# A smaller last group with paired down products, several chunks per bank, and identity products spread over the steps, in an LSTM with a mixture of experts

## The chip, the core and the metric

The kernel runs on one core of a Trainium2 chip. TensorE (PE) multiplies matrices and writes its results to PSUM, VectorE (DVE) and ScalarE (ACT) read them there, and SyncE (SP) issues most DMAs. Each engine works through its own instructions in the order in which the program issues them, and waits for the others by semaphores. The profile has two rows for TensorE: PE for the matmuls, and PEld for the loads of their stationary operand. An fp32 matmul is recorded as two passes, each with its own load, so a count of passes is twice the count of products.

The metric is the device time of one execution in microseconds (us). It is given as the median of several runs.

## What is computed

Two stages follow each other, each with a residual sum. The first is an LSTM over 1024 steps for two sequences of width 256:

```python
xW = einsum('ntd,dk->tnk', x, Wx) + b
def step((h, c), xw_t):
    a = xw_t + h @ Wh                       # 2 x 1024
    i, f, o = sigmoid(a[:, :256]), sigmoid(a[:, 256:512]), sigmoid(a[:, 512:768])
    g = tanh(a[:, 768:])
    c = f * c + i * g
    h = o * tanh(c)
x = x + hs
```

The second treats each of the 2 x 1024 tokens by itself. Two shared experts have a hidden width of 512, and eight routed experts a hidden width of 256. A router chooses two of the eight for each token:

```python
shared = sum_e (silu(x @ s_w1[e].T) * (x @ s_w3[e].T)) @ s_w2[e].T / 2
s = sigmoid(concat(x, cond) @ W_router.T)   # eight scores per token
idx = top_k(s + router_bias, 2)
gates = s[idx] / sum(s[idx])                # spread over the eight experts, zero elsewhere
routed = sum_e gelu(x @ r_w1[e].T) @ r_w2[e].T * gates[:, e]
x = x + (shared + routed) / 4
```

## The kernel before

**The recurrence.** One pass of the loop over `t` (L626) is one step. L641 to L651 issue 32 products of the last h with `Wh`, 64 columns each, on four column strips of the array (`ROWS` = 32): 64 passes. They accumulate onto the input part of the gates, which stands in the bank already. Then follow, for each of the two halves `m` of the hidden units, a transpose on DVE (L672), the sigmoids and the tanh on ACT (L675, L676), the cell on DVE (L679 to L684), its tanh on ACT (L692), and h on DVE (L695). The next step's first products need the first half of h.

**The input part.** `queue_inputs` (L531) queues products of x with `Wx` for 128 steps at a time (`XB`), and ACT moves them to SBUF with the bias. `inject` (L554) puts them into the gates' banks with identity products. A bank serves eight steps (`TH`). After the last burst of eight steps (`ahead`, L652) both banks of the next eight get their four identity products each: eight products, 16 passes, in one step.

**The experts as filler.** The tokens' work is done beside the recurrence, a group of steps later. `GROUPS` (L35) cuts the 1024 steps into seven groups of 128 and two of 64. When the last step of a group is done, `experts(t0, S)` (L255) queues its units on `fill.pe`. In the order of the queue they are: the router's scores, the up products of shared and routed experts, then per 128 tokens the identity product that brings in x with the shared down products, and the routed down products. A unit is mostly one matmul. `PACES` (L37) says in how many steps after the group's end its units are to be done. Each step runs at most `ROOM` = 2 of them behind its burst (L657, L658), less when fewer suffice for the due step:

```python
left = max(1, due - t)
done = fill.run_pe(min(ROOM - ahead, -(-len(fill.pe) // left)))
```

A unit that opens a PSUM bank runs only while a bank is free. There are two (`FILL_BANKS`, L38), and a bank is given back when the DVE operation that reads it last is issued (`let_go`). If a step has run fewer units than its room, padding follows (L659 to L664): products of the identity with itself, 256 columns, whose result nobody reads.

What ACT and DVE do for the experts stands in two more queues. `fill.run(fill.act, 1.0)` (L709) and `fill.run_dve(0.5)` (L718) take from them, in a step, as much as a written cost allows. The router's choice is some twenty small DVE operations in a queue `aside`, at a cost of `ASIDE` = 0.18 each.

**Chunks and banks.** An up product's bank holds two chunks of 128 hidden units, whatever the group's size: `w1` and `w3` of one chunk for the shared experts (`shared_up`, L363), and two chunks of `r1` for the routed ones (`routed_up`, L385).

**The end.** The last group ends with the last step, so nothing is left to hide its work. After L723 the queues are emptied, four more banks are lent to the filler (`fill.last`), and `drain` (L735) issues the group of 64 steps, 128 tokens. Its up products are cut into four strips of 32 output rows (`up_product`, L354). It has 8 shared and 16 routed down products of 256 columns, one identity product unit, and one sum on DVE per expert (`add_expert`, L446). An output DMA closes it.

Of the kernel before, what the change touches and what calls it, by code (L numbers as in the profile page):

```python
# [32 lines left out]
TOP_K = 2  # L33

GROUPS = [128] * 7 + [64] * 2  # L35

PACES = [128] * 6 + [84, 60, 0]  # L37
# [4 lines left out]
ROOM = 2  # L42
ASIDE = 0.18
# [67 lines left out]
def lstm_moe_kernel(  # L111
# [91 lines left out]
    nc.vector.tensor_scalar(ident_s, ident, 1.0 / SHARED, None, ALU.mult)  # L203
    rev = const.tile([P, E], F32, name="rev")
# [50 lines left out]
    def experts(t0, S):  # L255

        W = N * S
        NT = W // P
        mov = [x2[:, k, N * t0 : N * t0 + W] for k in range(K)]
        st = {}  # L260
        piece = 0.4 if W > P else 0.25

        def lhs(k, i):
            return toks(mov[k], i)

        def toks(a, i):
            return a[:, i * P : (i + 1) * P]


        def scores(i):  # L270
            if i == 0:
                st["lg"] = bank()[:, :, :E]
            for k in range(K):
                nc.tensor.matmul(
                    st["lg"][:, i, :], lhs(k, i), wr_sb[:, k, :],
                    start=(k == 0), stop=(k == K - 1),
                )
            if i == NT - 1:
                fill.to_dve(0.2, add_condition)

        def big(name):
            return route.tile([P, NT, E], F32, name=name)

        def small(name):
            return route.tile([P, NT], F32, name=name)

        def wide(a):
            return a.unsqueeze(2).to_broadcast([P, NT, E])

        def add_condition():  # L290
            st["z"] = big("z")
            nc.vector.tensor_add(
                st["z"], st["lg"][:, :NT, :], cond_lg.unsqueeze(1).to_broadcast([P, NT, E])
            )
            fill.let_go()
            fill.to_act(0.25, squash, lag=1)
# [6 lines left out]
        def choose():  # L303

            s = st["s"]
            rev_w = rev.unsqueeze(1).to_broadcast([P, NT, E])
# [3 lines left out]
                sel0, s, rb_sb.unsqueeze(1).to_broadcast([P, NT, E]), ALU.add))  # L310
# [39 lines left out]
            ]  # L350
            return ops


        def up_product(ps, half, w, c, k):  # L354

            rows = ROWS if fill.last and W <= P else P
            for r in range(0, P, rows):
                nc.tensor.matmul(  # L358
                    ps[r : r + rows, half, :W], w[:, k, c * P + r : c * P + r + rows], mov[k],
                    start=(k == 0), stop=(k == K - 1), skip_group_check=True,  # L360
                )

        def shared_up(c, i):  # L363
            if i == 0:
                if c == 0:
                    st["h_s"] = hidden.tile([P, NS * HS // P, N * P], F32, name="h_s")
                st["up"] = bank()
            up_product(st["up"], i // K, w3_sb if i // K else w1_sb, c, i % K)
            if i == 2 * K - 1:
                ps = st["up"]  # L370
                fill.to_act(0.4, lambda: shared_act(c, ps))

        def shared_act(c, ps):
            sg = work.tile([P, N * P], F32, name="sg")
            nc.scalar.activation(sg[:, :W], ps[:, 0, :W], AF.Sigmoid)
            y = work.tile([P, N * P], F32, name="y")
            fill.to_dve(piece, lambda: nc.vector.tensor_mul(y[:, :W], ps[:, 0, :W], sg[:, :W]))
            fill.to_dve(piece, lambda: shared_gate(c, ps, y))

        def shared_gate(c, ps, y):  # L380
            nc.vector.tensor_mul(st["h_s"][:, c, :W], ps[:, 1, :W], y[:, :W])
            fill.let_go()

        def routed_up(c2, i):
            if i == 0:  # L385
                if c2 == 0:
                    st["h_r"] = hidden.tile([P, E * HR // P, N * P], F32, name="h_r")
                st["up"] = bank()
            up_product(st["up"], i // K, r1_sb, 2 * c2 + i // K, i % K)
            if i == 2 * K - 1:  # L390
                ps = st["up"]
                fill.to_act(0.65, lambda: routed_act(c2, ps))

        def routed_act(c2, ps):
            er = work.tile([P, 2, N * P], F32, name="er")
            nc.scalar.activation(er[:, :, :W], ps[:, :, :W], AF.Erf, scale=RSQRT2)
            for half in range(2):
                fill.to_dve(piece, lambda half=half: routed_gate(c2, half, ps, er))

        def routed_gate(c2, half, ps, er):  # L400
            nc.vector.scalar_tensor_tensor(
                st["h_r"][:, 2 * c2 + half, :W], er[:, half, :W], 1.0, ps[:, half, :W],
                ALU.add, ALU.mult,
            )
            if half:
                fill.let_go()


        def shared_down(i, c):
            if c < 0:  # L410
                st["down"] = bank()
                x_kqj = st["down"][:, 0, :].rearrange("p (q k j) -> p k q j", q=Q, k=K)
                for k in range(K):
                    nc.tensor.matmul(
                        x_kqj[:, k], lhs(k, i), ident_s,
                        start=(k == 0), stop=False, skip_group_check=True,
                    )
                return
            last = c == NS * HS // P - 1
            nc.tensor.matmul(  # L420
                st["down"][:, 0, :], toks(st["h_s"][:, c, :], i), w2_sb[:, c, :],
                start=False, stop=last, skip_group_check=True,
            )
            if last:
                ps = st["down"]
                fill.to_dve(0.45, lambda: begin_sum(i, ps))

        def begin_sum(i, ps):
            st["acc", i] = work.tile([P, D], F32, name="acc")
            nc.vector.tensor_scalar(st["acc", i], ps[:, 0, :], SHARED, None, ALU.mult)  # L430
            fill.let_go()

        def routed_down(i, e2, j):
            if j == 0:
                st["down"] = bank()
            ps, half, h = st["down"], j // (HR // P), j % (HR // P)
            c = (2 * e2 + half) * (HR // P) + h
            nc.tensor.matmul(  # L438
                ps[:, half, :], toks(st["h_r"][:, c, :], i), r2_sb[:, c, :],
                start=(h == 0), stop=(h == HR // P - 1), skip_group_check=True,  # L440
            )
            if j == 2 * (HR // P) - 1:
                for half in range(2):
                    fill.to_dve(0.5, lambda half=half: add_expert(i, 2 * e2 + half, ps[:, half, :]), late=True)

        def add_expert(i, e, ps):  # L446
# [6 lines left out]
            if e == E - 1:  # L453
                t = t0 + i * (P // N)
                nc.sync.dma_start(out=out_tn[t : t + P // N], in_=acc)
# [3 lines left out]
        for c in range(NS * HS // P):  # L459
            units += [(int(i == 0), lambda c=c, i=i: shared_up(c, i)) for i in range(2 * K)]  # L460
        for c2 in range(E * HR // P // 2):
            units += [(int(i == 0), lambda c2=c2, i=i: routed_up(c2, i)) for i in range(2 * K)]
# [91 lines left out]
    def inject(ps, m, grp):  # L554
        blk, g = divmod(grp, XB // TH)
        assert all((blk, 4 * m + i, g * PAIR) in made for i in range(4))
        for q in range(Q):
            nc.tensor.matmul(  # L558
                ps[q * ROWS : (q + 1) * ROWS],
                pairs(blk)[:, 2 * m + q // 2, g].rearrange("p c r -> p (c r)"),  # L560
                ident[:, q % 2 * 64 : q % 2 * 64 + 64],
                start=True, stop=False, skip_group_check=True,
            )
# [59 lines left out]
    for m in range(K):  # L623
        inject(nxt[m][0], m, 0)
    due = 0
    for t in range(T):  # L626
        fill.step = t
        grp, u = divmod(t, TB)
        if t % TH == 0:
            cur, nxt = nxt, [gates_tile(m) for m in range(K)]  # L630
            ps, turned, busy = [a[0] for a in cur], [a[1] for a in cur], nxt[0][2]
            fresh = True
# [4 lines left out]
        if t == XB // 2:  # L637
            queue_inputs(1)

# [12 lines left out]
        ahead = t + 1 < T and t % TH == TH - 1  # L652
        if ahead:
            for m in range(K):
                inject(nxt[m][0], m, (t + 1) // TH)
            fresh = False
        left = max(1, due - t)  # L657
        done = fill.run_pe(min(ROOM - ahead, -(-len(fill.pe) // left)))  # L658
        for _ in range((ROOM if t < XB else 1) - done - ahead):  # L659
            nc.tensor.matmul(  # L660
                busy, ident, ident.unsqueeze(1).to_broadcast([P, 2, P]),
                start=fresh, stop=False, skip_group_check=True,
            )
            fresh = False  # L664
# [48 lines left out]
        if t == 2 * TB:  # L713
            lg = bank()[:, 0, :E]
            fill.banks -= 1
            fill.pe.extend((0, lambda k=k: condition_scores(lg, k)) for k in range(K))
        if u < TB - 1:
            fill.run_dve(0.5)  # L718
            continue
        residual(grp, int(grp == 0 or t - TB in ends), TB)  # L720
        if t in ends:
# [6 lines left out]
            if (t + 1) % XB == 0 and t + 1 + XB < T:  # L728
                queue_inputs((t + 1) // XB + 1)
# [82 lines left out]
```

## Time and profile before

The median of three runs is 2267.33 us (2264.34 to 2267.87).

| | |
|---|---|
| profiled execution, device time | 2267.39 us |
| its span, first to last instruction | 2265.6 us |
| mean granted TensorE clock | 0.998 |
| PE busy | 1923.0 us (85%) |
| PEld busy | 1417.4 us (63%) |
| DVE busy | 1571.0 us (69%) |
| ACT busy | 910.3 us (40%) |
| L644, the products with `Wh`, 65,536 passes | 1136.0 us of PE |
| L672, the transposes | 543.8 us of DVE, 266 ns each |
| L660, padding, 430 passes | 124.7 us of PE |
| L558, identity products, 2048 passes | 56.2 us of PE |

The busy share of PE is an average over 1024 steps that all have the same shape. Matmuls are pipelined, and the time of a row contains their latency, so 85% does not say that PE is full. What a change is worth must be read within one step, from where PE begins its filler to where the next burst can start, and from the steps that are longer than the others. The time from the last h to the end of the span, in which only the last group works, is read by itself.

### The profile page before, as it was taken

The numbers are of one execution on the slowest core, as the hardware profiler recorded it, in microseconds if no ns is written. First come the engines' busy times: TensorE is split into PE (matmuls) and PEld (weight loads), VectorE is DVE, ScalarE is ACT, GpSimd is POOL, SyncE is SP. The second block draws the span as 40 slices with busy tenths as digits, with TensorE's granted clock in tenths as the row PEclk, the third lists the DMA queues.
The fourth block names the chain that finished last, engine by engine and source line by source line (L and its number), as shares of the span: only waits on it lengthen the run. The fifth ranks groups of instructions, "written<-read, shape, count | busy, mean of one in ns | idle before, by whom it ended". The sixth has DMA issues, their size and how long they took to land.

```text
span 2265.6 us, 159453 instructions
## 1 busy us (share of the span) xinstructions
PE 1923.0 (85%) x70844; PEld 1417.4 (63%) x70844; DVE 1571.0 (69%) x10992; ACT 910.3 (40%) x6499; POOL 2.7 (0%) x9
## 2 busy tenths in 40 slices
PE   9999988888888888888888888888888888898888
PEld 6777765555655556555655556655566555676667
DVE  5666667766776667776677766776667766777776
ACT  4343344433444334443444434444343443343342
POOL 0000000000000000000000000000000000000000
PEclk9999999999999999999999999999999999999999
DMA  1221000000000000000000000000000000000000
GB/s 60 69 60 32 5 5 5 4 5 7 7 5 4 4 7 7 4 5 7 7 4 5 4 7 7 5 4 4 7 7 4 4 5 7 7 5 7 7 5 8
DMA packets 10707, 23.85 MB, mean 11 GB/s; under 512 B 2080, under 2 KB 7712, under 8 KB 10016
## 3 DMA queue, kind: packets, MB, share of 16 engines
q1 hardware_dynamic: 9728, 12.61, 1.9%
q8 instruction: 553, 9.06, 1.6%
q14 instruction: 138, 1.13, 0.2%
q10 hardware_dynamic: 288, 1.05, 0.1%
HBM read 11.56 MB, written 2.10 MB: 6 GB/s over the span
## 4 chain that ended last, share of the span: by engine, by line
PE 62%; DVE 34%; issue 3%; DMA 0%; SPq 0%; ACT 0%
PE ps L644 52%; DVE ps L672 10%; DVE c L684 9%; DVE results L679 7%; DVE seen L683 6%; PE ps L660 5%; DVE h L695 3%; PE ps_f L358 2%; PE ps_f L524 2%; PE ps_f L438 1%; PE ps_f L420 0%; PE ps L358 0%; DMA wh_sb<-in_wh_dram 0%; PE ps L558 0%; PE ps L438 0%
## 5 line engine op out<-in xcount | busy, mean ns | idle before, releaser
L644 PEld LDWEIGHTS ps<-wh_sb,h 128*32 128x32 f32 x65536 | 966.5, 110 | 727.7 <-DVE h L695 715.4
L644 PE MATMUL ps<-wh_sb,h 128*32 128x64 f32 x65536 | 1136.0, 221 | 331.7 <-DVE h L695 322.9
L672 DVE STREAM_TRANSPOSE ps<-ps 128x64 f32<-128x64 f32 x2048 | 543.8, 266 | 503.7 <-PE ps L644 433.9
L675 ACT ACTIVATE results<-ps 128x6 f32<-128x6 f32 x2048 | 362.9, 177 | 1106.0 <-DVE ps L672 1004.4
L695 DVE TENSOR_TENSOR h<-results,c 128x2 f32<-128x2 f32 x2048 | 313.6, 153 | 168.1 <-ACT c L692 168.0
L692 ACT ACTIVATE c<-c 128x2 f32<-128x2 f32 x2048 | 321.5, 157 | 218.0 <-DVE c L684 181.6
L684 DVE TENSOR_TENSOR_SCAN c<-results 128x4 f32<-128x4 f32 x2048 | 358.0, 175 | 0.0
L676 ACT ACTIVATE results<-ps 128x2 f32<-128x2 f32 x2048 | 340.3, 166 | 0.0
L683 DVE COPY seen<-results 128x2 f32<-128x2 f32 x2048 | 332.1, 162 | 0.0
L679 DVE TENSOR_TENSOR results<-results,c 128x2 f32<-128x2 f32 x2048 | 319.4, 156 | 0.0
L358 PE MATMUL ps_f<-x2T,w_sb 128*128 128x256 f32 (+2 forms) x608 | 168.7, 392 | 0.0
L358 PE MATMUL ps_f<-x2T,r_sb 128*128 128x256 f32 (+2 forms) x608 | 167.8, 390 | 0.0
L438 PE MATMUL ps_f<-r_sb,h_r 128*128 128x256 f32 x488 | 164.7, 426 | 0.0
L660 PE MATMUL ps<-ident 128*128 128x256 f32 x430 | 124.7, 408 | 0.8 <-issue 0.8
L358 PEld LDWEIGHTS ps_f<-x2T,w_sb 128*128 128x128 f32 (+1 forms) x608 | 79.2, 176 | 21.6 <-issue 0.3
L358 PEld LDWEIGHTS ps_f<-x2T,r_sb 128*128 128x128 f32 (+1 forms) x608 | 79.0, 176 | 21.5
L438 PEld LDWEIGHTS ps_f<-r_sb,h_r 128*128 128x128 f32 x488 | 74.4, 188 | 21.5
L660 PEld LDWEIGHTS ps<-ident 128*128 128x128 f32 x430 | 72.0, 189 | 16.8 <-issue 1.1
L420 PE MATMUL ps_f<-w_sb,h_s 128*128 128x256 f32 x240 | 81.5, 427 | 0.0
L524 PE MATMUL ps_f<-xT_sb,wx_sb 128*128 128x256 f32 (+2 forms) x384 | 78.6, 340 | 0.5 <-ACT inputs L513 0.3
L448 DVE SCALAR_TENSOR_TENSOR acc<-ps_f,gate,acc 128x256 f32<-128x256 f32 x122 | 58.3, 478 | 0.8 <-PE ps_f L438 0.7
L558 PE MATMUL ps<-ident,inputs 128*32 128x64 f32 x2048 | 56.2, 219 | 2.7 <-issue 2.0
(83 smaller groups left out, 498.9 us busy)
## 6 DMA issues: line engine op xcount, KB each, us to landing
r_sb<-in_r_w1T_dram SPq DMA_DIRECT2D x4, 512.0 KB, 3.8
r_sb<-in_r_w2T_dram SPq DMA_DIRECT2D x4, 512.0 KB, 4.5
out_dram<-acc SPq DMA_DIRECT2D x16, 128.0 KB, 2.8
xT_sb<-in_xT_dram SPq DMA_DIRECT2D x6, 256.0 KB, 2.9
wx_sb<-in_wx_dram ACTq DMA_DIRECT2D x2, 512.0 KB, 4.5
wh_sb<-in_wh_dram SPq DMA_DIRECT2D x2, 512.0 KB, 6.3
w_sb<-in_s_w1T_dram SPq DMA_DIRECT2D x2, 512.0 KB, 4.2
w_sb<-in_s_w3T_dram SPq DMA_DIRECT2D x2, 512.0 KB, 4.0
```

Source lines behind the costliest of these rows:

```text
L358: nc.tensor.matmul(ps[r : r + rows, half, :W], w[:, k, c * P + r : c * P + r + rows], mov[k], start=(k == 0), stop=(k == K - 1), skip_grou ...
L438: nc.tensor.matmul(ps[:, half, :], toks(st["h_r"][:, c, :], i), r2_sb[:, c, :], start=(h == 0), stop=(h == HR // P - 1), skip_group_check= ...
L644: nc.tensor.matmul(ps[m][q * ROWS : (q + 1) * ROWS], h_window(t, k, pair), wh_sb[:, k, w0 : w0 + 64], start=False, stop=(t % TH == TH - 1 ...
L660: nc.tensor.matmul(busy, ident, ident.unsqueeze(1).to_broadcast([P, 2, P]), start=fresh, stop=False, skip_group_check=True,)
L672: nc.vector.transpose(turned[m], ps[m])
L675: nc.scalar.activation(sgm[:, u, m, :, :, 1], gates[m][:, 0:3], AF.Sigmoid)
L676: nc.scalar.activation(gf[:, u, m, :, 0], gates[m][:, 3], AF.Tanh)
L679: nc.vector.tensor_mul(gf[:, u, m, :, 1], sgm[:, u, m, 2, :, 1], c_prev[m][:, :, 1])
L683: nc.vector.tensor_copy(seen[m], gf[:, u, m, :, 0])
L684: nc.vector.tensor_tensor_scan(c_new[m].rearrange("p n z -> p (n z)"), sgm[:, u, m, 0].rearrange("p n z -> p (n z)"), gf[:, u, m].rearrang ...
L692: nc.scalar.activation(cells[m][:, 2, :, 0], c_new[m][:, :, 1], AF.Tanh)
L695: nc.vector.tensor_mul(h_cols(t + 1)[:, m], sgm[:, u, m, 1, :, 1], cells[m][:, 2, :, 0])
```

## The change

Several edits come together.

**Groups.** A group of 32 steps is put in after the third group, and the last two groups have 64 and 32 steps. `XB` stays at 128, so the input products are queued at multiples of 128 steps, now apart from the groups' ends. The paces change with the groups: the last full group is due in 56 steps, the group of 64 in 31.

```diff
-GROUPS = [128] * 7 + [64] * 2
-PACES = [128] * 6 + [84, 60, 0]
+GROUPS = [128] * 3 + [32] + [128] * 4 + [64, LAST]
+PACES = [128] * 7 + [56, 31, 0]
-ROOM = 2
-ASIDE = 0.18
+ROOM = 3
+ASIDE = 0.19
```

**Identity products and padding.** Each step issues one of the eight identity products behind its filler. Padding is one product a step, and only in the eight steps of a bank whose first step had no filler. The input products of the first two blocks get due steps (12 and 128).

```diff
-        ahead = t + 1 < T and t % TH == TH - 1
-        if ahead:
-            for m in range(K):
-                inject(nxt[m][0], m, (t + 1) // TH)
-            fresh = False
         left = max(1, due - t)
-        done = fill.run_pe(min(ROOM - ahead, -(-len(fill.pe) // left)))
-        for _ in range((ROOM if t < XB else 1) - done - ahead):
+        done = fill.run_pe(min(ROOM, -(-len(fill.pe) // left)))
+        if t % TH == 0:
+            spare = not done
+        if spare and not done:
             nc.tensor.matmul(busy, ident, ...)
+        if t // TH + 1 < T // TH:
+            inject(nxt, t // TH + 1, t % TH)
...
-            fill.run_dve(0.5)
+            fill.run_dve(0.6)
```

**Several chunks per bank.** `up` takes the place of `up_product`, `shared_up` and `routed_up`. A bank holds `C` = 512 / W chunks for W tokens: two for a group of 128 steps, four for 64, eight for 32. All its products are 128 output rows by W columns, in the last group too. ACT and DVE then take half a bank at once, 256 columns, whatever W is.

```diff
+        C = 2 * 256 // W
+        def up(b, j):
+            i, k = divmod(j, K)
+            w, c = r1_sb, b * C - 2 * NS * HS // P + i
+            if c < 0:
+                w, c = (w1_sb, w3_sb)[i // (C // 2)], b * C // 2 + i % (C // 2)
...
+            nc.tensor.matmul(
+                ps[:, i, :], w[:, k, c * P : (c + 1) * P], mov[k],
+                start=(k == 0), stop=(k == K - 1), skip_group_check=True,
+            )
```

**The last group in pairs.** The last group has 64 tokens, half of the array's columns. Its scores are computed twice, for rows 0 to 63 and 64 to 127. Two chunks of a shared expert, or two experts, have their down products on the two halves of the array, and one DVE sum adds both with a gate per row. At the end a product with `fold` (two identities above each other) adds the two halves, ACT copies the result, and one DMA writes it.

```diff
+        def last_routed_down(e2):
+            ps = bank()
+            for h in range(HR // P):
+                for g in range(2):
+                    c = (2 * e2 + g) * (HR // P) + h
+                    nc.tensor.matmul(
+                        ps[g * W : (g + 1) * W, 0, :], st["h_r"][:, c, :W], r2_sb[:, c, :],
+                        start=(h == 0), stop=(h == HR // P - 1), skip_group_check=True,
+                    )
+            fill.to_dve(0.5, lambda: last_add(e2, ps), lag=0, late=True)
+
+        def last_add(e2, ps):
+            acc = st["acc", 0]
+            nc.vector.scalar_tensor_tensor(
+                acc, ps[:, 0, :], st["gates"][:, e2 : e2 + 1], acc, ALU.mult, ALU.add
+            )
+            fill.let_go()
+            if e2 == E // 2 - 1:
+                both = bank()[:W, 0, :]
+                nc.tensor.matmul(both, fold, acc, start=True, stop=True)
+                total = work.tile([P, D], F32, name="y")[:W]
+                nc.scalar.activation(total, both, AF.Copy)
+                nc.sync.dma_start(out=out_tn[t0 : t0 + S], in_=total)
```

`last_shared_down` does the same for the shared experts' eight chunks. One of the last two residual sums, which make the tokens from h, is issued before the last burst instead of behind it.

## Prediction

> **What bounds the kernel now.** I read the chain of waits first, then the matmuls in order of time, the table of waits, and last the granted clock in single windows. The chain:
>
> ```profile
> PE 62%; DVE 34%; issue 3%; DMA 0%; SPq 0%; ACT 0%
> ```
>
> Its largest line is the 64 passes of L644, which I call a burst: the product of one step with Wh. The recurrence h → burst → transpose → gates → h is the bound, and everything else has to fit beside it. In order of time, on PE:
>
> ```profile
> 2200.01 1.10 PE L644 MATMUL ps<-wh_sb,h 128*32 128x64 f32 x64 [0.19 <-DVE h L695]
> 2201.04 1.13 PE L420 MATMUL ps_f<-w_sb,h_s 128*128 128x256 f32 x4
> 2202.16 1.10 PE L644 MATMUL ps<-wh_sb,h 128*32 128x64 f32 x64
> ```
>
> Columns: start, time, engine, line, operation, operands, passes. A step takes 2.155 us. Filler can start 1.03 us into it, and two products of 256 columns (two passes each) still fit. Steps are this regular except in 45 places. The two writes of h in a step (L695) run from 11.4 to 2234.6, so 1023 steps take 2222.9 us; 1023 x 2.1545 is 2204.0, so about 18.3 us (summed over the 45) are lost. Where:
>
> ```profile
> PEld ps L644 <- issue: 10.7, 21, 0.9
> PEld ps L558 <- issue: 4.5, 12, 0.8
> ...
> 633.67 1.10 PE L644 MATMUL ps<-wh_sb,h 128*32 128x64 f32 x64 [0.43 <-DVE h L695]
> 634.59 0.41 PE L558 MATMUL ps<-ident,inputs 128*32 128x64 f32 x16
> 634.92 0.70 PE L358 MATMUL ps_f<-x2T,w_sb 128*128 128x256 f32 x2
> 635.83 1.09 PE L644 MATMUL ps<-wh_sb,h 128*32 128x64 f32 x61 [0.20 <-DVE h L695]
> 637.45 0.30 PE L644 MATMUL ps<-wh_sb,h 128*32 128x64 f32 x3 [0.54 <-issue]
> ...
> q8 instruction: 553, 9.06, 1.6%
> ```
>
> The burst stops three passes before its end with nothing to wait for. PE and PEld have 70,844 instructions each; 9.06 MB over them is 64 bytes each, and 553 packets make blocks of 16 KB, 256 instructions. All stops of this kind in L644 fall on the same place modulo 256: PE waits for the next block. Two regular steps hold about 264 instructions, so a block lasts some 4.2 us. The step before this stop had the eight identity products (L558, 16 passes): a block begun early in its burst is used up 2.8 us later, and its successor arrives 3.3 to 3.8 us after the begin. Two stretches are of another kind:
>
> ```profile
> 1425.50:1428.90 3.40, 2.37 (x88) 2.10 (x92) 2.42 (x19) 1.55 (x12) 0.00 (x0) 1.00 0.02 5
> 1428.90:1432.40 3.50, 3.50 (x103) 2.68 (x95) 1.46 (x12) 0.79 (x6) 0.00 (x0) 0.51 0.02 5
> 1705.40:1708.80 3.40, 3.25 (x77) 2.43 (x81) 1.60 (x14) 0.95 (x7) 0.00 (x0) 0.51 0.02 5
> ```
>
> The seventh number after the stretch's length (0.51) is the granted clock: twice PE ran at half speed for 3.4 us, each time after a step or two whose only filler was the 8-column router products (L274). The four steps touched lost 0.64, 0.42, 0.86 and 0.12, 2.04 us together. So 16.2 us belong to blocks of instructions: 5.5 before step 130, 10.7 later.
>
> **Identity products, one per step.** Their number stays. No step has 16 extra passes any more; with one filler product a step is 136 instructions, with two 140. I walked the block borders through the new order of PE. A border now moves back 16 to 24 instructions every two steps, and where it enters the head of a burst the next one lies at the end of the following burst, 3.0 us on. The trace has such pairs (steps 149, 181, 397) without a stop[...]. So the late 10.7 us go. Of the early 5.5 some 4 stay: there the weights' DMAs delay the blocks, and they are loaded at the same steps. **-12.2 us.** A rule speaks against this: the Trainium skill, "Runtime: NRT & Kernel Launch", section "Instruction fetch mechanics", has the crossing of a 16 KiB block mostly hidden. By it this part is worth nothing and the sum below ends at 2284.2; the row shows stops, so I take the row.
>
> **Up to three filler products per step** (ROOM 3, the new paces). The new order has 780 steps with one wide product, 92 with two, and 31 with three (or the router's four and one) plus an identity product, nearly all from 928 to 983, where 128 steps' work is due within 56 and two banks make a pattern of three, one, three, one. Another five or six (1015 to 1022) have three without identity product. What does a third cost? A late filler that holds the burst up:
>
> ```profile
> 670.59 0.70 PE L358 MATMUL ps_f<-x2T,r_sb 128*128 128x256 f32 x2
> 671.22 1.10 PE L644 MATMUL ps<-wh_sb,h 128*32 128x64 f32 x64
> ```
>
> From its start to the burst: 0.63 us, with h ready 0.12 earlier. A further product adds two passes of 0.216 (L420's 16 passes take 3.46 in the chain). Three: 1.03 + 0.63 + 4 x 0.216 = 2.52, and 0.04 for the identity product (16 passes of L558 take 0.41), 2.56: 0.41 over 2.155. 31 x 0.41 + 5 x 0.37 + 0.2 = **+14.9 us**. Below: nothing, if h were late as well, but h waits for the burst. Two products and an identity product end at 1.03 + 0.63 + 0.43 + 0.04 = 2.13 and fit, with 0.02 to spare; above: 0.05 for each of 92 steps, 4.6.
>
> **Less padding.** L660's padding (215 products) becomes 108, and none follows in eight steps whose first had a filler. 27 steps have only burst and identity product (12 to 15, 916 to 919, 985 to 991, twelve single ones); in 486 to 511 the extra group of 32 steps adds one 64-column product a step. The skill, "TensorE: Matmul & The Clock Gate", section "Why this matters for your kernels", warns of PE gaps over some 3 us only; no gap here is longer than about 1.2, so by it padding is worth nothing and the sum is 2267.5. The rows show half clock after mere bursts with short gaps. A window of 3.4 us spans 1.6 steps; it is as poor as the two seen when it holds little more than one burst, about one in three in a bare stretch: 2.5 of the 7 or 8 windows there, 1.5 to 2 of 16 in 486 to 511, 2 beside router products as now. 6.5 windows x 1.02 - 2.04 = **+4.6 us**; ends: -1 and +9.
>
> **DVE and ACT.** The budget 0.6 lets a 256-wide operation and a small one share a gap. Before the transposes DVE is idle 0.57; the wide one fills 0.34, the sum 0.40, two small ones 0.30: at most 0.54, hidden. Fewer, wider operations: nothing. DMAs and SP: one output more, nobody waits. The first identity product in eight steps now waits for an older product of PE itself; the next burst stands behind it, but that product is long done: nothing. One of the last two residual sums (0.14 on DVE) moves into the last step's gap.
>
> **The end.** Before: last h at 2234.76, span end 2265.6: 30.85 us. After, counted from the last h: the group of 64 is not done when the recurrence ends. Four of its products wait for a bank that a DVE sum frees behind h (0.6), and take 1.9 before the router's start (before: 0.35 after h); ups begin at 3.1 instead of 0.87. 64 products of 64 columns follow: nearest row L274, 8 columns in 0.112 a pass (weight load bound), 128 x 0.112 = 14.3, as long as now (14.7). Identity 0.6, then twelve pairs instead of 24 products at 0.43, 5.2 instead of 10.4; pairs of 64 columns are not in the trace, the burst's 64 passes of 53 ns stream in 0.875 four abreast, so I take full overlap (without: +5.2). Then a sum 0.7, fold product 0.7, ACT copy 0.45, and 3.15 as now from there to the end: 3.1 + 14.4 + 0.6 + 5.2 + 0.7 + 0.7 + 0.45 + 3.15 = 28.3. **-2.6 us.**
>
> **Sum.** -12.2 + 14.9 + 4.6 - 2.6 = +4.7. The profiled execution took 2267.39 (span 2265.6), as the median 2267.33 does: **2272.1**, slower by 0.21%. A difference under 0.2% (4.5 us) can't be told from none.
>
> **Rivals.** (a) The clock stays up, since a burst each 2.2 us is activity enough: 2272.1 - 4.6 = 2267.5, no difference. For it: only two windows in 1024 steps fell. Against: those fell with no gap over 1.2 us. (b) The other side: the third product costs little, as its passes overlap with the change to the burst's narrow weights; at 0.1 a step 3.6 instead of 14.9, 2260.8. It decides from below 0.17 a step. Against: the held burst above. (c) The block stops move to other steps instead of going: up to +12, 2284; halfway 2278. For it: three-product steps shift the borders again. (d) Pairs don't overlap: 2277.3.
>
> **Chances.** Forecast 0.46, (a) 0.26, (b) 0.12, (c) 0.1, (d) 0.06. As the forecast is near the bound, a quarter of its share lies within 0.2%, and some of (a) on each side: faster 0.13, same 0.32, slower 0.55. Range 2261 to 2280: from (b) to halfway (c); its own range 2267 to 2276.
>
> **What would show it.** PE <- issue at L717 near nothing after step 130; bursts 2.56 apart from 928 to 983; half clock in 985 to 991; 27 to 29 us from the last h to the end. It is wrong if bursts there stay 2.155 apart, or the stops go on.

## The result, and the profile after

The changed kernel takes 2280.66 us (median of 5 executions, 2274.82 to 2282.06); the kernel before, run beside it, 2267.87 (2264.34 to 2272.75). The ratio is 1.0048, with a 95% interval of 1.0036 to 1.0061: slower by 8 to 14 us, where 4.7 were forecast. The median lies 0.7 us above the stated range of 2261 to 2280, and outside the forecast's own 2267 to 2276. The profiled execution is the longest of the five, 2282.06 us with a span of 2280.3; it stands 14.7 us above the profiled execution of before (2267.39). That difference is taken apart below.

I cut the trace of each kernel at the first pass of every burst. A step is then the time from one burst to the next, and its excess is what it has over the regular 2.1545 us. Every step is put into one class:

| us of excess (steps) | before | after | difference | forecast |
|---|---|---|---|---|
| half clock | 2.0 (5) | 11.5 (17) | +9.5 | +4.6 |
| three and more filler products, burst held up by 0.25 or more | - | 14.5 (36) | +14.5 | +14.9 |
| before step 130, other | 6.4 | 4.2 | -2.2 | -1.5 |
| stops from step 130 on, over 0.1 each | 10.7 (25) | 2.4 (12) | -8.3 | -10.7 |
| small delays, all other steps | 0.4 (863) | 4.5 (832) | +4.1 | 0 |
| last h to the end of the span | 30.85 | 27.86 | -3.0 | -2.6 |
| until the first burst | 8.8 | 8.9 | +0.1 | 0 |
| sum | | | +14.7 | +4.7 |

The chain of waits after has almost the same shares as before, so it doesn't show the difference:

```profile
PE 61%; DVE 36%; issue 3%; DMA 0%; SPq 0%; ACT 0%
```

The table of waits does (line, what was waited for: us in total, times, longest). Before it had 10.7 us in 21 waits for "issue" on the burst's weight loads; now:

```profile
PEld ps L628 <- issue: 266.9, 803, 0.7
...
PEld ps L717 <- issue: 3.0, 5, 1.4
```

The stops in the burst have shrunk. The large new row at L628 is no loss: it is the weight load of the identity product, which has nothing to do while the filler ahead of it streams. (In experiment 6, which has the same order here, this row is 309.1; in experiment 10, with the identity product ahead of the filler, it is 0.3.) The matmuls in order of time, in the crowded stretch, show the third product (columns as before, PE only):

```profile
2037.29 1.10 PE L717 MATMUL ps<-wh_sb,h 128*32 128x64 f32 x64 [0.22 <-DVE h L767]
2038.32 1.56 PE L379 MATMUL ps_f<-x2T,w_sb 128*128 128x256 f32 x6
2039.81 0.24 PE L628 MATMUL ps<-ident,inputs 128*32 128x64 f32 x1
2039.82 0.26 PE L717 MATMUL ps<-wh_sb,h 128*32 128x64 f32 x3
2039.89 0.22 PE L628 MATMUL ps<-ident,inputs 128*32 128x64 f32 x1
2039.90 1.11 PE L717 MATMUL ps<-wh_sb,h 128*32 128x64 f32 x61
2040.93 0.70 PE L379 MATMUL ps_f<-x2T,w_sb 128*128 128x256 f32 x2
2041.56 0.30 PE L628 MATMUL ps<-ident,inputs 128*32 128x64 f32 x2
2042.05 1.10 PE L717 MATMUL ps<-wh_sb,h 128*32 128x64 f32 x64 [0.18 <-DVE h L767]
```

Two bursts lie 2.53 us apart where three products (6 passes) stand between them, and 2.23 where one does. The burst at 2039.82 shows no wait for h: it was held up by PE's own work. One more thing is to be seen, which becomes important below: the second pass of the identity product (2039.89) comes after the first three passes of the next burst.

The other new loss, again in order of time:

```profile
2166.12 1.10 PE L717 MATMUL ps<-wh_sb,h 128*32 128x64 f32 x64 [0.94 <-DVE h L767]
2167.04 0.28 PE L628 MATMUL ps<-ident,inputs 128*32 128x64 f32 x2
2168.28 1.82 PE L717 MATMUL ps<-wh_sb,h 128*32 128x64 f32 x64 [0.96 <-DVE h L767]
2169.87 0.42 PE L628 MATMUL ps<-ident,inputs 128*32 128x64 f32 x2
2171.14 1.93 PE L717 MATMUL ps<-wh_sb,h 128*32 128x64 f32 x64 [0.85 <-DVE h L767]
```

and the granted clock (seventh number after the stretch's length) in windows there:

```profile
2161.60:2165.00 3.40, 2.23 (x132) 2.07 (x132) 2.66 (x16) 0.95 (x7) 0.00 (x0) 1.00 0.02 5
2165.00:2168.40 3.40, 1.49 (x83) 1.17 (x79) 2.36 (x20) 1.58 (x12) 0.00 (x0) 1.00 0.14 46
2168.50:2171.90 3.40, 2.55 (x97) 2.31 (x89) 1.40 (x11) 0.79 (x6) 0.00 (x0) 0.50 0.01 2
```

From step 985 to 991 there are bursts and identity products and nothing else; such steps, without filler and padding, are called bare below. At 2168.5 the clock falls to half, the burst takes 1.8 to 1.9 us instead of 1.1, and this lasts for 17 us, into the steps whose filler has begun: 3.7 of the 11.5 us of the table fall in steps 992 to 994. In all the clock fell at 42.0, 1468.7, 2001.2 and 2168.5, for 6.8, 3.4, 6.8 and 17.1 us. Three of the four lie in or just behind the bare steps 12 to 15, 916 to 919 and 985 to 991, the other beside the router products of steps 671 to 673. The five executions tell the same by their mean clock: 0.999 took 2274.82 us, 0.998 2277.26, 0.994 and 0.995 2280.66 and 2280.71, 0.993 2282.06. Between the ends of this row that is 1.2 us for each 0.001, which points to 2273.6 at full clock (a line through all five: 1.1 and 2274.4).

The end, as the chain of waits has it (start, duration, what):

```profile
2252.62 0.40 DVE acc L462
...
2253.07 1.99 PE ps_f L452 x8
2255.07 0.34 PE ps L280 x8
2255.41 3.72 PE ps_f L379 x32
...
2270.31 1.83 PE ps L484 x16
2272.15 0.86 PE ps L496 x8
2273.01 0.86 PE ps_f L496 x8
2273.88 1.76 PE ps L496 x15
```

The leftover products of the group of 64 wait for DVE's sum (0.4) and take 2.0, the ups run from 2255.4 to 2269.8, and the twelve pairs (48 passes) take 5.3 us in all.

### The profile page after: what moved, and what is told of

Same layout as the page of the kernel before. It is cut to its first block, busy times and chain, and to the rows that moved or that the text cites. A ratio compares the mean times of both kernels' runs of the same rounds, so it can differ in the third digit from the quotient of the medians.

```text
span 2280.3 us, 158749 instructions
## 1 busy us (share of the span) xinstructions
PE 2069.2 (91%) x70436; PEld 1510.9 (66%) x70436; DVE 1570.6 (69%) x10993; ACT 908.3 (40%) x6487; POOL 2.7 (0%) x9
## 4 chain that ended last, share of the span: by engine, by line
PE 61%; DVE 36%; issue 3%; DMA 0%; SPq 0%; ACT 0%
PE ps L717 51%; DVE ps L744 10%; DVE c L756 10%; DVE results L751 7%; DVE seen L755 6%; PE ps_f L379 3%; DVE h L767 3%; PE ps_f L452 2%; PE ps L628 1%; PE ps_f L434 1%; PE ps_f L594 1%; PE ps L379 0%; DMA wh_sb<-in_wh_dram 0%; PE ps_f L428 0%; PE ps L730 0%
## 5 line engine op out<-in xcount | busy, mean ns | idle before, releaser
L717 PEld LDWEIGHTS ps<-wh_sb,h 128*32 128x32 f32 x65536 | 977.8, 110 | 348.8 <-DVE h L767 342.2
L628 PEld LDWEIGHTS ps<-ident,inputs 128*32 128x32 f32 x2048 | 141.6, 108 | 306.4 <-issue 266.9
L628 PE MATMUL ps<-ident,inputs 128*32 128x64 f32 x2048 | 305.4, 232 | 0.1
L452 PE MATMUL ps_f<-r_sb,h_r 128*128 128x256 f32 (+1 forms) x512 | 163.7, 418 | 1.3 <-DVE acc L462 1.3
L379 PEld LDWEIGHTS ps_f<-x2T,r_sb 128*128 128x128 f32 x608 | 90.2, 188 | 23.4 <-issue 0.5
L379 PEld LDWEIGHTS ps_f<-x2T,w_sb 128*128 128x128 f32 x608 | 89.6, 191 | 22.4 <-issue 0.5
L452 PEld LDWEIGHTS ps_f<-r_sb,h_r 128*128 128x128 f32 (+1 forms) x512 | 79.2, 185 | 23.6 <-DVE acc L462 1.7
L434 PE MATMUL ps_f<-w_sb,h_s 128*128 128x256 f32 (+1 forms) x256 | 81.4, 417 | 0.1
L730 PE MATMUL ps<-ident 128*128 128x256 f32 x216 | 76.5, 436 | 0.5 <-issue 0.5
L462 DVE SCALAR_TENSOR_TENSOR acc<-ps_f,gate,acc 128x256 f32<-128x256 f32 (+1 forms) x128 | 61.1, 477 | 1.2 <-PE ps_f L452 1.0
```

The costliest lines, as they stand in the source:

```text
L379: nc.tensor.matmul(ps[:, i, :], w[:, k, c * P : (c + 1) * P], mov[k], start=(k == 0), stop=(k == K - 1), skip_group_check=True,)
L452: nc.tensor.matmul(ps[:, half, :], toks(st["h_r"][:, c, :], i), r2_sb[:, c, :], start=(h == 0), stop=(h == HR // P - 1), skip_group_check= ...
L628: nc.tensor.matmul(banks[m][0][q * ROWS : (q + 1) * ROWS], pairs(blk)[:, 2 * m + q // 2, g].rearrange("p c r -> p (c r)"), ident[:, q % 2 ...
L717: nc.tensor.matmul(ps[m][q * ROWS : (q + 1) * ROWS], h_window(t, k, pair), wh_sb[:, k, w0 : w0 + 64], start=False, stop=(t % TH == TH - 1 ...
```

## Experiments

Eleven kernels, in four batches; each batch had the kernel before run beside it (medians 2268.15, 2266.59, 2267.49 and 2266.17). Times are medians; of experiments 4 and 8 there is one execution each. What a trace shows is of one execution.

**1. Only the identity products.** In the kernel before, eight at once become one per step:

```diff
-        ahead = t + 1 < T and t % TH == TH - 1
-        if ahead:
-            for m in range(K):
-                inject(nxt[m][0], m, (t + 1) // TH)
...
+        if t // TH + 1 < T // TH:
+            inject(nxt, t // TH + 1, t % TH)
```

> The kernel before with one part of the change: one identity product in every step instead of eight in one of eight steps (groups, paces, two products per step at most, padding and the end as before). Theory 1 (eight at once use a block of instructions up before its successor is there): of the 10.7 us that steps after 130 lose to stops in the burst about 1.8 stay, of 6.4 us before step 130 about 4.2 stay, half clock stays 2.0: 2267.4 - 11 = 2256 us, last h to the end 30.8 as before. Rival 2 (the stops only move to other steps): 2264 to 2268, with 8 us or more of stops after 130. Rival 3 (the identity product holds the next burst up in the 160 steps that have two products, 0.05 each): 2264, with two-product steps 2.20 us long.

2263.89 us against 2268.15, ratio 0.9982 (0.9973 to 0.9990): a gain of 4 us, not 11. (Before step 128 the kernel before fills a step up to two products with padding, later up to one.) The padding here may begin its accumulation behind identity products of the same bank; by the Trainium skill, "PSUM — Partial Sum Buffer", section "The four PSUM rules", a product that begins an accumulation clears the written marks of the whole bank in the rows that it writes, so part of the input products is missing from the gates; no trace here shows those marks. The work of a step is that of the expectation. In the trace the stops after step 130 are 4.4 us (15 steps), not 1.8; before step 130 it loses 8.3, with 0.07 behind 28 of the 111 steps of two padding products and an identity product, nearly all of them with the first quarter of a bank; the small delays are 3.5. Half clock doesn't occur in it (2.0 in the profile of before). So each of the three theories is partly right: the stops shrink by 6.3, they do move (to 171, 308, 398 and others), and the identity product has a price.

**2. Padding in every step without filler.**

```diff
-            spare = False
+            fresh = True
...
-        if t % TH == 0:
-            spare = not done
-        if spare and not done:
+        if not done:
             nc.tensor.matmul(
                 busy, ident, ident.unsqueeze(1).to_broadcast([P, 2, P]),
-                start=(t % TH == 0), stop=False, skip_group_check=True,
+                start=fresh, stop=False, skip_group_check=True,
             )
+            fresh = False
```

> The changed kernel with one padding product in every step that has no other filler product (in the changed kernel none in 27 of those). Theory 1 (bare steps bring the half clock): of 11.5 us lost in half-clock steps under 2.5 stay (the steps with router products alone), the rest unchanged: 2282.1 - 9 = 2273 us profiled, mean clock 0.998 or more in every run, and the runs within 4 us of each other. Rival 2 (half clock comes from elsewhere, the heavier steps 928 to 983 for one): half clock stays in or near steps 985 to 994 and the median stays 2277 to 2282.

2273.49 us (15 executions, 2271.26 to 2276.95), every one with a mean clock of 0.999 or 1.000. As in the first experiment, part of the input products is missing from the gates. Where the changed kernel ran bare, now (first the matmuls of a step, then the clock in steps 989 and 990, which ran at half clock there):

```profile
2157.85 0.70 PE L728 MATMUL ps<-ident 128*128 128x256 f32 x2
2158.48 0.30 PE L628 MATMUL ps<-ident,inputs 128*32 128x64 f32 x2
2158.97 1.10 PE L717 MATMUL ps<-wh_sb,h 128*32 128x64 f32 x64 [0.20 <-DVE h L766]
```

```profile
2165.40:2168.80 3.40, 3.17 (x133) 2.49 (x134) 1.81 (x13) 0.98 (x9) 0.00 (x0) 1.00 0.03 7
```

The long steps were as before (36, 14.5 us), so they don't bring the half clock: rival 2 falls. The time also agrees with the 2273.6 to 2274.4 that the five executions of the changed kernel pointed to.

**3. At most two products per step.**

```diff
-ROOM = 3
+ROOM = 2
```

> The changed kernel with ROOM 2: at most two filler products per step. Steps 985 to 991 are then no longer bare (12 to 15 and 916 to 919 still are), and 24 products of 256 columns and 12 of 128 of the group of 64 steps are left for after the last h, where it was 4. Theory 1 (the third product costs 0.40 us a step): 14.5 us of long steps go, 6 us of half clock go, the end grows by 20 x 0.43 + 12 x 0.22 = 11.3 us to 39.2: 2282.1 - 9.2 = 2273 us. Rival 2 (the long steps come from the identity product or the waits of banks): bursts stay 2.5 us apart in some of 928 to 983, and the time is 2285 or more. Rival 3 (the left over products cost more at the end, each bank waiting for DVE): end over 45 us, 2279 or more.

2270.30 us (2265.84 to 2271.78) against 2268.15, ratio 1.0006 (0.9998 to 1.0014). No step is held up by 0.25 by a third product any more; the end grows from 27.9 to 37.3 us. In its crowded stretch:

```profile
2040.60 1.11 PE L717 MATMUL ps<-wh_sb,h 128*32 128x64 f32 x64
2041.64 1.13 PE L379 MATMUL ps_f<-x2T,w_sb 128*128 128x256 f32 x4
2042.70 0.24 PE L628 MATMUL ps<-ident,inputs 128*32 128x64 f32 x1
2042.77 0.25 PE L717 MATMUL ps<-wh_sb,h 128*32 128x64 f32 x2
```

Bursts are 2.17 us apart with two products (4 passes) and an identity product between them. So the 14.5 us are the third product's. The profiled execution shows no half clock during the recurrence, though steps 12 to 15 and 916 to 919 are still bare; others of its executions had a mean clock of 0.996 to 0.998. The same order of instructions doesn't fall each time.

**4. The last group without pairs.**

```diff
-        two = t0 + S == T
+        two = False
```

> The changed kernel with the last group of 32 steps going the way of the other groups: each expert's down product for 64 tokens alone, gates on 64 rows, no fold product at the end. Theory 1 (the two products of a pair run beside one another): 24 products of 0.43 us take 10.4 instead of 5.2, the fold product and the ACT copy behind it (1.1) go: the last h to the end 32 us instead of 27.9. Rival 2 (pairs run one after the other or nearly): the end is 27 us or less.

2284.60 us. The last h to the end is 32.5 us (27.9 with pairs), so the pairs bring 4.7 and run beside one another. The 24 products in the trace (start, duration, passes):

```profile
2268.10 3.62 PE L434 MATMUL ps<-w_sb,h_s 128*64 128x256 f32 x16
2271.55 1.89 PE L452 MATMUL ps<-r_sb,h_r 128*64 128x256 f32 x8
2273.28 1.89 PE L452 MATMUL ps_f<-r_sb,h_r 128*64 128x256 f32 x8
2275.01 3.62 PE L452 MATMUL ps<-r_sb,h_r 128*64 128x256 f32 x16
```

16 passes take 3.45 from start to start here; in the changed kernel 16 passes of pairs take 1.83.

Up to the last group the experiments 2 and 4 and the changed kernel differ in padding at most, and 4 not at all. After step 130 their stops sum to 6.1, 4.7 and 2.4 us, in partly different steps. So the stops vary between executions, and the changed kernel's profile shows a low case.

**5. One identity product and at most one padding product per step,** with the padding's accumulation begun in the first step of each eight. The diff is against the kernel of experiment 1:

```diff
-        for _ in range((ROOM if t < XB else 1) - done):
+        if t % TH == 0:
+            spare = done < 2 or t < XB
+        if spare and (not done or t % TH == 0):
...
-                start=fresh, stop=False, skip_group_check=True,
+                start=(t % TH == 0), stop=False, skip_group_check=True,
```

> The kernel before with one identity product per step, as in the first experiment, and two edits of the padding: at most one padding product per step (there were two per step before step 128), its accumulation begun in the first step of each eight. Theory 1 (two padding products and an identity product in one step held the early bursts up by 0.07, and the stops of the instruction blocks shrink but stay): before step 130 about 4.3 us lost where the first experiment had 8.3; stops after it 4.4 (3 to 6); two-product steps 2 us in all; last h to the end 31: 2260 us. Rival 2 (the early losses come from the weights' DMAs whatever is beside them): 2264 as in the first experiment, with 8 us before step 130.

2265.01 us against 2266.59, ratio 0.9994 (0.9985 to 1.0003): no gain. The early loss went down to 5.3 and the stops were 3.4, but the small delays rose to 7.5. The trace has most of them in one place. Behind two products and an identity product of the first quarter of a bank, the next step is too long by 0.043 us (median of 132 steps). These are the first and fifth steps of each eight; in 92 of the first ones a filler and a padding product stand together.

**6. The changed kernel, packed anew.** Room by width, and the due time of the last group of 128 later:

```diff
-PACES = [128] * 7 + [56, 31, 0]
+PACES = [128] * 7 + [62, 31, 0]
-ROOM = 3
+ROOM = 2
...
+    def cost(self, unit):
+        return unit[2] if len(unit) > 2 else 1
...
-            (int(j == 0), lambda b=b, j=j: up(b, j))
+            (int(j == 0), lambda b=b, j=j: up(b, j), 0.5 if W <= P else 1)
...
-            spare = not done
-        if spare and not done:
+            spare = done < 2
+        if spare and (not done or t % TH == 0):
```

> The changed kernel with its filler packed anew: a step's room is 2 products of 256 columns, the up products of a group of 64 steps or less (128 columns and fewer) count half, so a step takes two wide or four narrow ones; the group of 128 that ends with step 927 is due in 62 steps instead of 56; the first step of each eight gets a padding product beside up to one filler, so later steps of the eight can have one too. Theory 1 (the loss of the changed kernel is 14.5 us of third wide products and about 10 of half clock, the end's 3 us gain stays): no step after 130 over 2.45 us but for stops; half clock none; stops 4.8, early 4.3, the remaining small delays 3.8; end 28.3: 2259 us, mean clock 0.999 or more in every run. Rival 2 (four narrow products hold the burst up as three wide ones do, or the group of 64 is left over for the end): 2266 or more, end over 33 us.

2263.35 us against 2266.59, ratio 0.9987 (0.9978 to 0.9996); 2259 was expected. The long steps are gone, the clock is 0.999 or 1.000 in every execution, and the end is 27.9. Four narrow products cost little; bursts are 2.19 apart (2204.59 and 2206.78 are the starts of two):

```profile
2204.59 0.26 PE L724 MATMUL ps<-wh_sb,h 128*32 128x64 f32 x3
...
2205.67 1.16 PE L386 MATMUL ps_f<-x2T,r_sb 128*128 128x128 f32 x8
2206.76 0.24 PE L635 MATMUL ps<-ident,inputs 128*32 128x64 f32 x1
2206.78 0.26 PE L724 MATMUL ps<-wh_sb,h 128*32 128x64 f32 x3
```

What is missing to the expected time are small delays of 8.3 where 3.8 were expected. Again they stand mostly behind the first quarter, in 84 first steps of eight behind one filler and one padding product.

**7. Eight identity products at once in the changed kernel.**

```diff
-        if t // TH + 1 < T // TH:
-            inject(nxt, t // TH + 1, t % TH)
+        if t + 1 < T and t % TH == TH - 1:
+            for i in range(K * Q):
+                inject(nxt, t // TH + 1, i)
```

> The changed kernel with the identity products eight at once in the last of eight steps, as before, all else as changed. Theory 1 (this is what stopped the bursts): stops after step 130 return from 2 to 5 us to about 10, the small delays of one- and two-product steps (4.3) go to about 1: net +3 to +5 against the changed kernel's 2280.7, 2284 us at the same clock. Rival 2 (an identity product in each step costs as much as the stops it saves): 2280 or less.

2288.85 us (4 executions, 2284.47 to 2293.58, mean clock 0.987 to 0.994). In the profile, half clock apart, stops after step 130 are 9.3 us, before it 7.2 are lost, small delays 0.2: 16.7 together, where the changed kernel has 11.1 and experiment 4, the same instructions but for the end, 13.3. So spreading brings 3 to 6 us (2 against experiment 2, which has 14.4), and theory 1 holds in size too, within what the stops vary. The rest of the time is clock, at a new place: between 1084.8 and 1129 us, in steps 494 to 512, whose filler has 64 columns only. With an identity product in each of them (the changed kernel's profile, experiment 4's) they stayed at full clock. Four executions are few for that; it is seen, not settled.

**8. No padding at all.**

```diff
-            spare = not done
+            spare = False
```

> The changed kernel without any padding product: 135 steps have no filler (27 in the changed kernel), above all 12 to 63, 80 to 127, 916 to 927 and 985 to 991. Theory 1 (in a stretch of such steps every clock window after the first is at half speed, 0.85 us a step as in steps 16, 920 and 990): 119 steps of long stretches, about 100 us in place of the 11.5 now: 2365 us, single steps without filler unharmed. Rival 2 (a window falls one time in three, as I forecast): 2310. Rival 3 (gaps this short do nothing): 2275.

2323.57 us (one execution). 181 us of the recurrence ran at half clock, which cost 52.0 us in 73 steps. The clock (seventh number) in two stretches of bare steps, the first spared and the second not:

```profile
64.00:70.00 6.00, 3.60 (x198) 3.11 (x198) 3.59 (x29) 2.30 (x18) 0.00 (x0) 1.00 0.29 90
98.00:104.00 6.00, 4.33 (x145) 3.85 (x140) 2.70 (x20) 1.58 (x12) 0.00 (x0) 0.50 0.12 46
```

It lies between theory 1 and rival 2: in a long bare stretch the clock falls and stays down for up to 82 us at a time, but not always and not at once. It also comes back inside such a stretch: steps 17 to 19 were slow, the bare steps 20 to 29 at full clock, later ones slow again; and steps 985 to 991 were spared. Rival 3 is out.

**9. The quarters of the identity product in another order,** in the packed kernel:

```diff
-            inject(nxt, t // TH + 1, t % TH)
+            inject(nxt, t // TH + 1, [1, 2, 3, 0, 5, 6, 7, 4][t % TH])
```

> The packed kernel of the sixth experiment with the eight identity products in another order: the first of each eight steps does the second quarter of the rows of the bank instead of the first (the first quarter, with which each burst begins, comes fourth). In the runs so far the burst behind two filler products and an identity product of the first quarter starts a step that is 0.043 us too long (median), behind the other quarters 0.011 to 0.017; the sixth experiment has 84 steps with one filler, one padding product and the first quarter. Theory 1 (it is the quarter): those 84 steps lose 0.012 each, 2.6 us go: small delays of one- and two-product steps 4.5 to 5 instead of 7.5, 2263.3 - 2.6 = 2260.7 us. Rival 2 (it is the first step of eight, a new bank, whatever quarter): 2263, the delay of 0.043 stays with the first step.

2259.70 us (2258.74 to 2260.50) against 2267.49, ratio 0.9964 (0.9952 to 0.9977). I compare medians behind two products and an identity product, from experiment 6 to this one. Behind the first and fifth steps of each eight, which had the first quarter, the excess went from 0.043 to 0.028; behind the fourth and eighth, which have it now, from 0.013 to 0.071. So the cost goes with the quarter, and rival 2 falls. Where both products are filler, all of it goes (0.047 to 0.012, 43 steps); where one is padding, 0.030 of 0.043 stays (84 steps), and why is open. The gain in time is not the quarter's alone: the stops from step 130 on were 6.3 us in experiment 6's profile and are 3.1 here, while the regular step of this batch is longer (2.158 us, some 3 us in sum). The same place before (experiment 6) and now:

```profile
1243.84 0.59 PE L737 MATMUL ps<-ident 128*128 128x256 f32 x2
1244.37 0.24 PE L635 MATMUL ps<-ident,inputs 128*32 128x64 f32 x1
1244.43 0.25 PE L724 MATMUL ps<-wh_sb,h 128*32 128x64 f32 x2
1244.45 0.22 PE L635 MATMUL ps<-ident,inputs 128*32 128x64 f32 x1
```

```profile
1241.75 0.59 PE L737 MATMUL ps<-ident 128*128 128x256 f32 x2
1242.28 0.24 PE L635 MATMUL ps<-ident,inputs 128*32 128x64 f32 x1
1242.35 0.26 PE L724 MATMUL ps<-wh_sb,h 128*32 128x64 f32 x2
1242.36 0.22 PE L635 MATMUL ps<-ident,inputs 128*32 128x64 f32 x1
```

In both, the identity product's second pass comes among the burst's first passes.

**10. The identity product ahead of the filler,** in the packed kernel (the two lines moved to just behind the burst).

> The packed kernel with the identity product directly behind the burst, ahead of the filler. Theory 1 (an identity product just ahead of a burst is in the way of the burst's first passes): two-product steps lose 0.02 at most, their filler starting 0.02 to 0.04 later with 0.02 to spare: small delays 2 to 3 us instead of 7.5: 2259 us. Rival 2 (the filler that starts later holds up the burst as much): two-product steps lose 0.04 to 0.06 whatever the quarter, 130 x 0.04 and more at four narrow ones: 2264 to 2266.

2262.06 us (2259.94 to 2263.37) against 2267.49, ratio 0.9974 (0.9964 to 0.9985). Here the first identity product of a bank comes ahead of the padding that begins its accumulation, and part of the input products is missing from the gates. No burst is stretched: behind two products with one after them the excess is 0.003 whatever the quarter, as in every regular step of this batch. But steps of two products (filler and padding together) start the next burst 0.025 later than in experiment 9, those of three 0.04, of four narrow ones 0.06. Both theories hold, and against each other: what the burst wins, the late filler loses.

**11. Padding beside a filler only at need,** in the kernel of experiment 9:

```diff
-            spare = done < 2
+            spare = done < (2 if fill.work() < TH else 1)
```

> The ninth experiment's kernel (packed anew, quarters turned) with the padding product beside a filler product only where fewer than 8 products are queued, that is where the next steps would be bare: 8 steps instead of 84. Theory 1 (those steps lose 0.03 each behind their padding): small delays of one- and two-product steps 5 instead of 7.4, 2259.7 - 2.3 = 2257.4 us, no half clock but for a window beside the router products (672, 673, as the changed kernel had one), 1 us. Rival 2 (what those steps lose, others gain, or the block stops take the place): 2260. Rival 3 (fewer padding products bring the half clock back in 485, 544, 672, 800 and the 64-column steps 486 to 511): clock 0.997 or less in several runs, 2263.

2258.62 us (2256.22 to 2262.39) against 2266.17, ratio 0.9970 (0.9959 to 0.9980); small delays 5.0, as expected, and no half clock in the recurrence of the profiled execution (others had mean clocks down to 0.998). Its interval overlaps that of experiment 9. By their intervals both are faster than the kernel before by 5 to 11 us; the changed kernel is slower than it by 8 to 14.

## Why the prediction was right in kind and short in size

**Identity products (-12.2 forecast).** That eight at once stop the bursts was right: experiments 1 and 7 show it from both sides. The profiled execution has -10.5 (-2.2 early, -8.3 late). But the claim that the late stops go was wrong, and that they go on was one of the forecast's own signs of being wrong: they become smaller and less regular (2.4, 4.7 and 6.1 in three executions of nearly one order of instructions). I had three pairs of block borders without a stop as proof that such places don't stop; 25 stopped steps against hundreds of crossings is a rate, not a rule. What makes them vary is open, and so is whether the weights' DMAs delay the early blocks: the early loss was 2.8 to 8.3 us in experiments that load the same weights. Rival (c), that stops move, had part of the truth.

**"Two products and an identity product fit, with 0.02 to spare".** This term failed: I put it at nothing, with 4.6 as the upper end, and the small delays grew by 4.1 us, to 4.5. Of these, 2.2 stand behind the 123 steps of two products, and 1.5 behind 40 steps of three, where I had counted the hold-up alone. The sum of durations was not what was wrong. An identity product occupies a quarter of the array, and its second pass starts among the first passes of the next burst; behind two products that costs 0.043 us with the first quarter and about 0.012 with the others. The burst begins with the first quarter, which would explain the difference; no run tests that apart. This isn't in the trace of before, where eight such products stood in a row, ahead of the filler.

**Third product (+14.9).** 36 steps, 14.5 us: the row of the held burst gave the right price (the addends as written make 14.8), and experiment 3 took it away. Rival (b) is out.

**Less padding (+4.6).** The sign and the three bare stretches were right, the size was not: I counted 6.5 windows, one in three in a bare stretch. In this execution ten fell, nine of them in or behind the three bare stretches, and none in 486 to 511 or in the single steps. The windows aren't independent, as I had treated them: here the clock, once down, stayed down to the end of the stretch and beyond (five windows in a row from step 989 on), though experiment 8 shows that it can also come back. And a window costs more where filler has begun: step 992 lost 1.7 us, a bare step 0.83. At the median of the executions the price is about 7 us (2280.66 - 2273.5), and from 1 to 9 by the chance of the execution. So rival (a) is out. To allow no gaps over about 3 us, as the Trainium skill, "TensorE: Matmul & The Clock Gate", section "Why this matters for your kernels", advises, is not enough here: in the bare steps at full clock PE is idle for at most 0.97 us at a time, and padding is worth 7 us.

**The end (-2.6).** -3.0. The leftover products took 2.0, the ups 14.4, the pairs 5.3, near to what was written; experiment 4 excludes rival (d).

**DVE and ACT, DMAs.** Put at nothing, and nothing showed: the median step with one filler product is 2.154 us, as before.

Two errors had the same sign (4.9 for the clock, 4.1 for small delays); with 1.7 from the stops (10.5 for 12.2) they make up the forecast's shortfall of 10.0 against the profiled execution, to within 0.7. That the sum at full clock, some 2274, lies near the forecast of 2272.1 is in part luck: the small delays stand where the forecast had the clock.

## What to carry to other kernels

Price a new order of work by its most crowded and by its emptiest steps, not by its mean: here a third product in 36 steps (14.5 us) and no product in 15 steps (some 7 us) each cost more than the smaller last group with its pairs brought (3.0 us). Against the third product's cost stands that its work, put off, makes the end 9.4 us longer (experiment 3). When a recurrence leaves TensorE room, count filler by its time and not by its number, and keep the padding where the filler runs out. A small product that uses a part of the array belongs where the part is not the next one needed.

## What the runs showed of the hardware

- Half clock came with bursts of 1.1 us and a small product of 0.28 us every 2.15 us and idle gaps under 1 us. With one further product of 256 columns in each such step, all 15 executions of experiment 2 had a mean clock of 0.999 or 1.000, and the profiled one no half clock in the recurrence. It comes in multiples of 3.41 us, lasted up to 82 us, and differs from execution to execution of the same instructions.
- Stops at the blocks of instructions differ between executions too: 2.4, 4.7 and 6.1 us in sum for nearly the same order.
- Passes of a product of 32 columns of weights and of the burst behind it start interleaved (the traces above). Behind two other products, which quarter it uses decides between 0.012 and 0.043 us.
